# A two-layer graph network on one core: 36 instead of 28 groups of layer 1 take their rows from one-hot products, and ScalarE writes every fifth one-hot

## The chip, the core and the metric

The kernel runs on one core of one Trainium2 chip. The core has five engines that run their own instruction queues in order and wait for each other by semaphores: TensorE (PE, with its weight loads listed apart as PEld), VectorE (DVE), ScalarE (ACT), GpSimd (POOL) and SyncE (SP, which only issues transfers here). The metric is device time in microseconds (us) of one execution. Six executions of the kernel before took 3845.5 to 3851.33 us, with a median of 3848.85 us.

## What is computed

There are N = 12,500 nodes with 48 features and E = 200,000 edges, sorted by their target `dst`. Layer 0 is an edge network, layer 1 a sum of rectified messages, and each is added to its input and normalised over the features:

```python
x_i, x_j = x[dst], x[src]
h   = relu(concat([x_i, x_j, e32]) @ W1 + b1)
x   = layernorm(x + segment_sum(h @ W2 + b2, dst, N))          # layer 0
m   = relu(x[src] + e48)
x   = layernorm(x + (1 + eps) * x + segment_sum(m, dst, N))     # layer 1
```

What matters below is `x[src]` in layer 1: 200,000 rows of 48 floats, taken from 12,500 nodes in an order that the edges give.

## The kernel before, in words

The edges are cut into 391 groups of 512 (`NCHUNK` groups of `TPC` = 4 tiles of 128 edges). Layer 0 is a loop over the 391 groups, then layer 1 is another one. The instructions are written out in a fixed order by hand (`run`): in step k each stage handles group k minus its offset, and every engine meets its instructions in that order.

In layer 1 a step k issues, in this order:

- `fetch1(k+5)`: four indirect transfers on POOL's queue (L201), one for each tile, each of which brings 128 rows of `x1_dram` into the tile `xs`. The pool `cats` has 10 buffers for `xs` (`AHEAD + 5`), so the gathers of a group can start once the add of the tenth gathered group before it has been done.
- `fill1(k+2)`: DVE makes the 48-wide one-hot `hot` of the target (L302); SP loads the edge features `e48c` every fifth group.
- `sum1(k-1)`: PE multiplies messages with `hot` (L323), DVE adds the result to the window of sums `agg` (L318).
- every 28 groups a `finish1`: the sums of 896 nodes are turned, added and normalised (L331 to L357), mostly on DVE.
- `message1(k)`: DVE adds rows and edge features (`m`, L495), ACT applies the relu (`msg`, L497).
- `lead1(k)`: takes one portion from the generator `products()`.

`products()` replaces the gathers of some groups, the list `PE_GROUPS`; `fetch1` skips these. It works on two of these groups at a time (`BATCH` = 2, so `tiles` = 8 tiles). `place` makes `which` in PSUM, a bf16 tile of 128 x 1024: for each edge the number of its source's block of 128 nodes, at the row of the node within the block, and 0 elsewhere (8 DVE operations `which_e` at L515, 8 PE transposes at L520). Then, for each of the 98 blocks of nodes, `select` compares `which` with the block's number in one DVE operation of 128 x 1024 (`o`, L525), and `multiply` runs 8 matmuls of that one-hot with the block's nodes `xp` (L530), which are kept in SBUF as three bf16 pieces. The three sums (`ph`, `pm`, and one of two buffers `pt`; the other `pt` holds `which`) are opened and closed by matmuls of zeros (L538) and summed by three DVE reduces (`made`, L570). A portion is `BPS` = 4 selects for the next blocks and the multiplies of the blocks selected in the portion before. The one-hots `o` have 2 x `BPS` buffers.

With 98 blocks in portions of 4 there are 25 portions and one more for the end of the pair: 26 steps for two groups, and `EVERY` = 13 groups lie from one product group to the next. The first is group 26, the last group 377; layer 1 gathers 363 groups.

Of the kernel before, what the change touches and what calls it, by code (L numbers as in the profile page):

```python
# [24 lines left out]
F32 = mybir.dt.float32  # L25
I32 = mybir.dt.int32
BF16 = mybir.dt.bfloat16
AF = mybir.ActivationFunctionType
# [3 lines left out]
P = 128  # L32
Q = 128
# [7 lines left out]
NT = -(-N // Q)  # L41
# [14 lines left out]
AHEAD = 5  # L56
NW = 4
EC = 5
FIRST = 26
EVERY = 13  # L60
NPE = 28
BATCH = 2
PIECES = 3
BPS = 4

PE_GROUPS = [FIRST + EVERY * i for i in range(NPE)]
assert PE_GROUPS[-1] < NCHUNK and NPE % BATCH == 0

# [29 lines left out]
@with_exitstack  # L98
def gnn_kernel(
    ctx: ExitStack,  # L100
    tc: tile.TileContext,
    x: bass.AP,
    src: bass.AP,
    dst: bass.AP,
    e32: bass.AP,
    e48: bass.AP,
    w1: bass.AP,
    b1: bass.AP,
    w2: bass.AP,
    b2: bass.AP,  # L110
    eps: bass.AP,
    out: bass.AP,
):
    nc = tc.nc
    flag_pool = ctx.enter_context(tc.tile_pool(name="flag", bufs=1))
    dram = ctx.enter_context(tc.tile_pool(name="dram", bufs=1, space=bass.MemoryType.DRAM))
    flag = flag_pool.tile([1, 1], I32, name="flag")
    with ExitStack() as fast:
        windowed(fast, tc, dram, flag, x, src, dst, e32, e48, w1, b1, w2, b2, eps, out)
    misfit = nc.values_load(  # L120
        flag, engines=[mybir.EngineType.PE, mybir.EngineType.DVE, mybir.EngineType.Activation,
                       mybir.EngineType.Pool, mybir.EngineType.SP],
        min_val=0, max_val=2 * P,
    )
    with tc.If(misfit > 0), ExitStack() as slow:
        general(slow, tc, dram, x, src, dst, e32, e48, w1, b1, w2, b2, eps, out)


def windowed(ctx, tc, dram, flag, x, src, dst, e32, e48, w1, b1, w2, b2, eps, out):
    nc = tc.nc  # L130
    const = ctx.enter_context(tc.tile_pool(name="const", bufs=1))
    onehots = ctx.enter_context(tc.tile_pool(name="onehots", bufs=2 * BPS))
    cats = ctx.enter_context(tc.tile_pool(name="cats", bufs=AHEAD + 5))
    echunk = ctx.enter_context(tc.tile_pool(name="echunk", bufs=3))
    work = ctx.enter_context(tc.tile_pool(name="work", bufs=2))
# [23 lines left out]
    for t in wcats:  # L159
# [22 lines left out]
                   allow_small_or_imprecise_dtypes=True)  # L182
    iota_w = const.tile([P, W], F32, name="iota_w")
    nc.gpsimd.iota(iota_w, pattern=[[1, W]], base=0, channel_multiplier=0,
                   allow_small_or_imprecise_dtypes=True)
# [6 lines left out]
                   allow_small_or_imprecise_dtypes=True)  # L192
# [7 lines left out]
    def gather(t, table, g, j):  # L200
# [9 lines left out]
    base = const.tile([1, NCHUNK], F32, name="base")  # L210
# [10 lines left out]
        off, base, starts, op=ALU.subtract  # L221
# [22 lines left out]

    part = const.tile([P, NPE, TPC], F32, name="part")
    block = const.tile([P, NPE, TPC], F32, name="block")

    def split_src():
        first = FIRST * TPC
        some = src_i[:, first : first + (NPE - 1) * EVERY * TPC].rearrange(  # L250
            "p (i c) -> p i c", c=EVERY * TPC
        )[:, :, 0:TPC]
        last = src_i[:, PE_GROUPS[-1] * TPC : (PE_GROUPS[-1] + 1) * TPC]
        bits = node.tile([P, NPE, TPC], I32, name="bits")
        for op, by, plus, to in (
            (ALU.bitwise_and, Q - 1, 0.0, part), (ALU.logical_shift_right, 7, 1.0, block)
        ):
            nc.vector.tensor_scalar(bits[:, : NPE - 1, :], some, by, None, op0=op)
            nc.vector.tensor_scalar(bits[:, NPE - 1, :], last, by, None, op0=op)
            nc.vector.tensor_scalar(to, bits, plus, None, op0=ALU.add)  # L260
# [244 lines left out]
    tiles = BATCH * TPC  # L505
# [3 lines left out]
    def place(first):  # L509

        which = psum.tile([Q, tiles, P], BF16, name="pt", bufs=2)
        for i in range(BATCH):
            which_e = work.tile([P, TPC, Q], BF16, name="which_e")
            for j in range(TPC):
                nc.vector.tensor_scalar(  # L515
                    which_e[:, j, :], iota_q, part[:, first + i, j : j + 1],
                    block[:, first + i, j : j + 1], op0=ALU.is_equal, op1=ALU.mult,
                )
            for j in range(TPC):
                nc.tensor.transpose(which[:, i * TPC + j, :], which_e[:, j, :], ident16)  # L520
        return which

    def select(which, b):
        o = onehots.tile([Q, tiles, P], BF16, name="o")
        nc.vector.tensor_scalar(o, which, float(b + 1), None, op0=ALU.is_equal)  # L525
        return o

    def multiply(ps, o, b):
        for k in range(tiles):
            nc.tensor.matmul(  # L530
                ps[k // PER][:, k % PER, :], o[:, k, :], xp[:, b, :, :],
                start=False, stop=False, skip_group_check=True,
            )

    def edge_of(ps, start):
        for t in ps:
            n = t.shape[1] * PIECES * D
            nc.tensor.matmul(  # L538
                t.rearrange("p k c d -> p (k c d)"), zeros[:, :P], zeros[:, :n],
                start=start, stop=not start,  # L540
            )
# [4 lines left out]
    def products():  # L546

        for first in range(0, NPE, BATCH):
            due = PE_GROUPS[first]
            which = place(first)  # L550
            ps = [
                psum.tile([P, min(PER, tiles - k * PER), PIECES, D], F32, name=name,
                          bufs=2 if name == "pt" else 1)
                for k, name in enumerate(SUMS)
            ]
            edge_of(ps, True)
            last = []
            for b in range(0, NT, BPS):
                now = [(b + i, select(which, b + i)) for i in range(min(BPS, NT - b))]
                for c, o in last:  # L560
                    multiply(ps, o, c)
                last = now
                yield due
            for c, o in last:
                multiply(ps, o, c)
            edge_of(ps, False)
            xs = work.tile([P, tiles, D], F32, name="made")
            for k, t in enumerate(ps):
                n = t.shape[1]
                nc.vector.tensor_reduce(  # L570
                    xs[:, k * PER : k * PER + n, :], t.rearrange("p k c d -> p k d c"),
                    AX.X, ALU.add,
                )
            for i in range(BATCH):
                made[PE_GROUPS[first + i]] = xs[:, i * TPC : (i + 1) * TPC, :]
            yield due

    work1 = products()

    def lead1(k):  # L580
# [217 lines left out]
```

## Time and profile before

| what | value |
|---|---|
| median of six executions | 3848.85 us |
| the profiled execution | 3844.86 us |
| its span, first to last instruction | 3843.1 us |
| mean granted TensorE clock | 0.785 of full |
| layer 0 gathers, first and last start | 1564, 7.5 and 1969.9 us |
| layer 1 gathers, first and last start | 1452, 1990.5 and 3826.9 us |
| DVE selects (L525) | 1372, 677 ns each |

The page gives the busy time of each engine, its course over 40 slices of the span, and the groups of instructions by line. The timeline lists instructions in order of time with the idle time before each and what ended it. PE's busy time is modelled from pipelined matmuls and is not PE at its peak. The granted clock comes in stretches at full and at half speed, so a mean of 0.8 is a mixture of the two.

### The profile page before, as it was taken

How to read it: one execution, taken by the hardware profiler on the slowest of the kernel's cores; microseconds unless marked ns; L12 is line 12 of the kernel's file. 1: busy time of each engine (PE TensorE's matmuls, PEld its weight loads, DVE VectorE, ACT ScalarE, POOL GpSimd, SP SyncE). 2: the span in 40 equal slices, each digit the busy share in tenths (PEclk: the TensorE clock that was granted, in tenths of full speed). 3: DMA queues.
4: the chain of work that ended last, by engine and by line, in shares of the span. 5: the costliest groups of instructions: out<-in, count | busy, mean ns of one | idle time of the engine just before them, and what ended most of it. 6: DMA issues, size and time to landing. Idle time of an engine off the chain costs nothing. (4 is left out here: it accounts for less than half of the span.)

```text
span 3843.1 us, 67581 instructions
## 1 busy us (share of the span) xinstructions
PE 2857.3 (74%) x23396; PEld 2210.4 (58%) x23396; DVE 1896.1 (49%) x4618; ACT 565.2 (15%) x1329; POOL 2883.9 (75%) x3025
## 2 busy tenths in 40 slices
PE   7888888888888888888876766767676676667631
PEld 4555555556555556555556656656666665666531
DVE  3333333333333333333356766767677677767731
ACT  2222212212212212212110000000000000000000
POOL 7777777777777777777767777777777777777776
PEclk8787777787778777777778788878888888878865
DMA  2222222222212222222212222222222222212221
GB/s 71 43 45 48 43 45 46 47 40 49 48 39 45 49 41 47 49 37 47 41 40 43 45 43 38 55 45 43 38 50 43 38 50 49 44 33 55 45 43 28
DMA packets 293005, 171.68 MB, mean 45 GB/s; under 512 B 109664, under 2 KB 292400, under 8 KB 292656
## 3 DMA queue, kind: packets, MB, share of 16 engines
q0 software_dynamic: 96512, 74.31, 13.2%
q1 hardware_dynamic: 179248, 84.31, 8.1%
q10 hardware_dynamic: 16896, 8.69, 0.8%
q8 instruction: 185, 3.03, 0.3%
q14 instruction: 164, 1.34, 0.1%
HBM read 154.45 MB, written 12.62 MB: 43 GB/s over the span
## 5 line engine op out<-in xcount | busy, mean ns | idle before, releaser
L201 POOL DMA_INDIRECT cat<-in_x_dram,src_i x1564 | 1486.9, 951 | 481.4 <-issue 342.0
L201 POOL DMA_INDIRECT xs<-x_dram,src_i x1452 | 1395.1, 961 | 462.0 <-issue 339.1
L530 PEld LDWEIGHTS <-o 128*128 128x128 bf16 x10976 | 848.6, 112 | 22.9 <-DVE o L525 0.6
L525 DVE TENSOR_SCALAR o<-pt 128x1024 bf16<-128x1024 bf16 x1372 | 848.5, 677 | 5.4 <-PE pt L520 5.4
L419 DVE COPY cat_t<-pt 128x512 f32<-128x512 f32 x391 | 270.2, 691 | 898.4 <-PE pt L417 898.4
L323 PE MATMUL pa<-hot,msg 128*48 128x48 f32 x3128 | 257.5, 235 | 557.9 <-ACT msg L497 557.4
L417 PEld LDWEIGHTS pt<-ident,cat 128*128 128x128 f32 x1564 | 265.5, 176 | 631.6 <-DMA cat<-in_x_dram,src_i 365.2
L424 PE MATMUL ph<-cat_t,wcat 128*128 128x512 f32 x782 | 579.0, 831 | 0.8 <-DVE cat_t L419 0.8
L323 PEld LDWEIGHTS pa<-hot,msg 128*48 128x48 f32 x3128 | 204.5, 145 | 639.6 <-ACT msg L497 618.1
L417 PE MATMUL pt<-ident,cat 128*128 128x128 f32 x1564 | 389.9, 349 | 238.3 <-DMA cat<-in_x_dram,src_i 235.2
L530 PE MATMUL ph<-xp,o 128*128 128x144 bf16 x4116 | 565.3, 255 | 0.0
L530 PE MATMUL pm<-xp,o 128*128 128x144 bf16 x4116 | 562.8, 254 | 0.0
L432 PE MATMUL pm<-w_sb,h 128*128 128x48 f32 x3128 | 538.7, 326 | 1.3 <-ACT h L426 1.3
L432 PEld LDWEIGHTS pm<-w_sb,h 128*128 128x128 f32 x3128 | 484.8, 237 | 28.1 <-ACT h L426 2.4
L426 ACT ACTIVATE h<-ph,b_sb 128x512 f32<-128x512 f32 x391 | 269.0, 688 | 1370.5 <-PE ph L424 1351.9
L530 PE MATMUL pt<-xp,o 128*128 128x144 bf16 x2744 | 453.9, 253 | 0.0
L495 DVE TENSOR_TENSOR m<-xs,e48c 128x192 f32<-128x192 f32 x363 | 132.9, 366 | 539.6 <-DMA xs<-x_dram,src_i 539.1
L497 ACT ACTIVATE msg<-m 128x192 f32<-128x192 f32 x391 | 141.8, 363 | 1606.2 <-DVE m L495 1606.2
L323 PE MATMUL pa<-cat,msg 128*48 128x48 f32 x3128 | 263.6, 239 | 33.0 <-DVE msg L434 30.5
L323 PEld LDWEIGHTS pa<-cat,msg 128*48 128x48 f32 x3128 | 210.5, 149 | 113.1 <-issue 55.9
L434 DVE TENSOR_TENSOR msg<-pm,b_sb 128x192 f32<-128x192 f32 x391 | 139.4, 356 | 236.7 <-PE pm L432 234.6
L318 DVE TENSOR_TENSOR agg<-agg,pa 48x48 f32 x782 | 151.4, 194 | 175.2 <-PE pa L323 124.1
(79 smaller groups left out, 1064.6 us busy)
## 6 DMA issues: line engine op xcount, KB each, us to landing
e48c<-in_e_dram SPq DMA_DIRECT2D x78, 480.0 KB
cat<-in_x_dram,src_i POOLq DMA_INDIRECT x1564
e32c<-in_e_dram SPq DMA_DIRECT2D x78, 320.0 KB
xs<-x_dram,src_i POOLq DMA_INDIRECT x1452
wcat<-a SPq DMA_DIRECT2D x391, 24.0 KB
a<-a ACTq DMA_DIRECT2D x14, 256.0 KB
a<-a ACTq DMA_DIRECT2D x14, 192.0 KB
x_seg<-in_x_dram SPq DMA_DIRECT2D x14, 168.0 KB
```

The costliest lines, as they stand in the source:

```text
L201: nc.gpsimd.indirect_dma_start(out=t, out_offset=None, in_=table, in_offset=bass.IndirectOffsetOnAxis(ap=src_i[:, g * TPC + j : g * TPC + ...
L318: nc.vector.tensor_tensor(cols, cols, pa, op=ALU.add)
L323: nc.tensor.matmul(pa, msg[:, j, :], hot[:, j, :], start=j == 0, stop=j == TPC - 1)
L417: nc.tensor.transpose(pt[:, j, :], cat[g][:, j, :], ident[:P, :P])
L419: nc.vector.tensor_copy(cat_t, pt)
L424: nc.tensor.matmul(ph, wcats[g % NW], h[g], start=True, stop=True)
L426: nc.scalar.activation(t, ph, AF.Relu, bias=b1_sb)
L432: nc.tensor.matmul(pm[:, j, :], h[g][:, j, :], w2_sb, start=True, stop=True)
L434: nc.vector.tensor_tensor(msg, pm, b2_sb[:, None, :].to_broadcast([P, TPC, D]), op=ALU.add)
L497: nc.scalar.activation(msg, m, AF.Relu)
L525: nc.vector.tensor_scalar(o, which, float(b + 1), None, op0=ALU.is_equal)
L530: nc.tensor.matmul(ps[k // PER][:, k % PER, :], o[:, k, :], xp[:, b, :, :], start=False, stop=False, skip_group_check=True,)
```

## The change

Three constants give the product groups: the first is group 20, one in ten follows, 36 in all (20, 30, ... 370). A portion has 5 blocks instead of 4, so the one-hots have 10 buffers. For blocks 2, 7, ... 97 (20 of 98) ACT writes the one-hot in two operations, the square of `which` minus the block's number and then relu(1 - square), by way of one buffer `square`. The bias comes from a new constant `less`, filled by one POOL iota. The portion that ended a pair is gone: the last multiplies and the reduces now stand in the same step as the `place` and first selects of the next pair, so that a pair takes 20 steps.

```diff
-FIRST = 26
-EVERY = 13
-NPE = 28
+FIRST = 20
+EVERY = 10
+NPE = 36
-BPS = 4
+BPS = 5
+BY_ACT = 2
...
+    less = const.tile([Q, NT], F32, name="less")
+    nc.gpsimd.iota(less, pattern=[[-1, NT]], base=-1, channel_multiplier=0,
+                   allow_small_or_imprecise_dtypes=True)
+
     def select(which, b):
         o = onehots.tile([Q, tiles, P], BF16, name="o")
+        if b % BPS == BY_ACT:
+            square = work.tile([Q, tiles, P], BF16, name="square", bufs=1)
+            nc.scalar.activation(square, which, AF.Square, bias=less[:, b : b + 1])
+            nc.scalar.activation(o, square, AF.Relu, bias=1.0, scale=-1.0)
+            return o
         nc.vector.tensor_scalar(o, which, float(b + 1), None, op0=ALU.is_equal)
         return o
...
                 made[PE_GROUPS[first + i]] = xs[:, i * TPC : (i + 1) * TPC, :]
-            yield due
```

## The prediction

> **What bounds the kernel now.** I read the page first, its busy line and its slices.
>
> ```profile
> PE 2857.3 (74%) x23396; PEld 2210.4 (58%) x23396; DVE 1896.1 (49%) x4618; ACT 565.2 (15%) x1329; POOL 2883.9 (75%) x3025
> DVE  3333333333333333333356766767677677767731
> POOL 7777777777777777777767777777777777777776
> ```
>
> POOL is at the same 7 tenths in both layers, though PE and DVE change by a factor of two between them. That speaks for a fixed pace on POOL. The groups of instructions confirm it:
>
> ```profile
> L201 POOL DMA_INDIRECT xs<-x_dram,src_i x1452 | 1395.1, 961 | 462.0 <-issue 339.1 <-DMA xs<-x_dram,src_i 86.6 <-DVE o L525 15.5
> L525 DVE TENSOR_SCALAR o<-pt 128x1024 bf16<-128x1024 bf16 x1372 | 848.5, 677 | 5.4 <-PE pt L520 5.4
> L426 ACT ACTIVATE h<-ph,b_sb 128x512 f32<-128x512 f32 x391 | 269.0, 688 | 1370.5 <-PE ph L424 1351.9
> ```
>
> A gather takes 0.96 us and is followed by 0.3 us of issue, whatever it is put down to; a POOL that waited for others would show long gaps. In layer 1 the starts run from 1990.53 to 3826.92: 1836.4 us over 1451 intervals, 1.2656 each, 5.062 for a group. Next, the list of waits: DVE's add waits for the gathered rows in 270 of 363 cases.
>
> ```profile
> DVE m L495 <- DMA xs<-x_dram,src_i: 539.1, 270, 4.2
> ```
>
> So DVE has slack, and the question is how much. The timeline of DVE shows it where DVE is behind and works without a pause, and at the change from one pair to the next:
>
> ```profile
> 2284.63 0.35 DVE L495 TENSOR_TENSOR m<-xs,e48c 128x192 f32<-128x192 f32 x1
> 2284.90 2.48 DVE L525 TENSOR_SCALAR o<-pt 128x1024 bf16<-128x1024 bf16 x4
> 2287.30 0.34 DVE L302 TENSOR_TENSOR hot<-iota_w,rel 128x192 f32<-128x192 f32 x1
> 2287.56 0.19 DVE L318 TENSOR_TENSOR agg<-agg,pa 48x48 f32 x1
> 2287.68 0.34 DVE L495 TENSOR_TENSOR m<-xs,e48c 128x192 f32<-128x192 f32 x1
> ```
> ```profile
> 2585.65 0.39 DVE L495 TENSOR_TENSOR m<-xs,e48c 128x192 f32<-128x192 f32 x1 [2.26 <-DMA xs<-x_dram,src_i]
> 2585.96 0.59 DVE L570 TENSOR_REDUCE made<-ph 128x144 f32<-128x432 f32 x1
> ...
> 2587.36 0.34 DVE L302 TENSOR_TENSOR hot<-iota_w,rel 128x192 f32<-128x192 f32 x1
> ...
> 2591.51 2.13 DVE L515 TENSOR_SCALAR which_e<-iota_q,part,block 128x128 bf16<-128x128 f32 x8
> 2594.03 2.48 DVE L525 TENSOR_SCALAR o<-pt 128x1024 bf16<-128x1024 bf16 x4 [0.39 <-PE pt L520]
> ```
>
> A step with four selects lasts 3.05 us from add to add, against 5.06 for the gathers of a group. The four selects overlap: 2.40 from the first's start to `hot`, 0.60 apart.
>
> **The change, part by part.** *Gathers.* 363 gathered groups become 355: 32 gathers less, 32 x 1.2656 = **40.5 us less on POOL**, the path that sets the end. This is the whole gain.
>
> *The iota* (`less`) stands on POOL before layer 1's first gather. The nearest row, an iota of 128x128, took 0.24 us, and POOL idles 19.72 us there until the last of `x1_dram` is written. Nothing; uncovered it would cost 0.3.
>
> *ACT instead of DVE for 20 of 98 blocks.* DVE still has 4 selects a step. The built program's semaphores decide what ACT's part does to it: the Square waits for the DVE select before it, and the next DVE select waits for the Square, because both engines read the one PSUM tile `which`. So ACT does not work beside DVE here: DVE stands still during the Square, and behind the waiting select stand the fourth select, `hot`, `agg` and the next add, for which ACT's relu, PE's sums and, ten gathered groups on, POOL wait. Only the Relu lies beside DVE.
>
> The price of a Square has no row. The nearest in kind is L426, PSUM to SBUF with a pointer bias, 0.688 for 512 elements; the copies from PSUM took 0.597 for 512 and 0.491 for 384, a slope of 0.83 ns an element. From L426: 0.688 + 512 x 0.00083 = 1.112. Low end, from the copy: 0.597 + 0.424 = 1.021. High end, by the slope from L497 (192 elements, 0.363) to L426, 1.016 ns: 1.208. I take 1.112, since L426 differs only in length and type. The handovers are 0.09 (add to relu, DVE to ACT) and 0.03 (ACT to DVE), both in the chain of waits at the end. A step then grows by 0.09 + 1.11 + 0.03 and by 0.08 of lost overlap (0.677 less 0.60): 1.32. **DVE's step becomes 4.37.**
>
> The Trainium skill, "PSUM — Partial Sum Buffer", section "PSUM bank collisions raise a hardware error", speaks against this change: accesses of two engines to one bank and quadrant have to be kept apart by semaphores, two reads too. No row of before shows two engines reading one tile, so this trace can't confirm it; if reads could lie beside each other, the sum would end at the 40.5 gained. The skill's "ScalarE: Activation LUTs", section "What ACT_TABLE_LOAD costs", gives about 280 ns plus 0.833 ns an element for a pointer bias, an estimate of 1.133 for the Square; L426 at 0.688 agrees with it within 3%, and the sum below would be 7 us longer by it.
>
> *A round of 20 steps on DVE.* Eighteen steps of 4.37 are 78.6. The step with blocks 95 to 97 has two DVE selects and nothing behind its Square: 3.05 - 2 x 0.60 = 1.85. The next, which ends a pair and begins another: the reduces wait for PE, PE for block 97 from ACT. Square and Relu are through 3.85 after the add before, so 2.0 after this one; 8 matmuls and the zeros add about 1.1: 3.1. Then 1.40 for the reduces (2585.96 to 2587.36), 2.52 to the first select (2591.51 to 2594.03), and 5 blocks with `hot` and `agg`: 2.40 + 0.38 + 1.32 = 4.10. In all 11.1. Round: **91.6**, plus a `finish1` every 28 steps, 5.4 and 5.9 in two places of the timeline, 5.6 taken. POOL needs 18 x 5.062 = 91.1. DVE, which had some 30% to spare, becomes as slow as POOL or slower.
>
> *What becomes of it.* Call lag the time from landing to add. Before, group 0 has 7.7 (its last gather starts at 1994.4, lands 2.5 later, its add starts at 2004.6). Six portions stand before it, each 1.32 longer: 15.6. Fourteen steps take off 0.69 each, the short step 3.2, the long one adds 6.1: 8.8 at group 16. From there to 341, the last group before the final round thins out: DVE 16 x 91.6 + 5 x 4.37 + 12 finishes x 5.6 = 1555; POOL gathers 325 - 33 = 292 groups, 1478. The lag would reach 86. But 10 buffers hold it: a group's gathers begin ten groups, 50.6, after those of the group whose buffer they take, of which 3.8 to its last start, 2.5 to landing and 0.4 for the add are used. Room 44. So **POOL stands still for 42 us**. After step 355 there are no selects and the rest is gathered at the old pace.
>
> *Waits for PE.* In the 113 steps of before without idle time ahead of the add, DVE lost 8.4 us ahead of `agg`, 0.07 each. PE gets 40 instead of 32 matmuls a step, but 4.37 instead of 3.05 us for them: 0 to 0.07, or 0 to 24 us over 325 steps. I take 7.
>
> **Sum: -40.5 + 42 + 7 = +8.5.** The profiled execution's 3844.9 would become 3853; against the median, which is 4 us above it, **3857 us**.
>
> **The rivals.** *Gain kept.* If Square and selects lay beside each other, a DVE round is 66.5 plus 4 for finishes, far under 91.1, no lag grows and the time is 3848.85 - 40.5 = 3808. For it: ACT is 15% busy, and only one Square a step is in question. Against it: the semaphores. Short of that, 329 Squares count from the start to group 341, so the Square would have to cost 0.15 less, 0.96, below my low end, for POOL never to wait. Chance 0.15.
>
> *PE at half clock* (L530, slower). The matmuls follow each other at 62 ns at full clock and 120 at half. A round is 784 of them, 20 sums at 0.56 and about 2 us of the rest: 62 us at full, over 120 at half. It passes DVE's 95 when the granted clock is under 0.65; at 0.6 a round is 103 and 17 rounds cost 200, less the room, about +120, 3970. For it: the throttle granted 0.73 to 0.83 in layer 0's middle, with PE busier. Against: layer 1 had 0.82 with PE waiting for DVE and rows, and its stretch from 2600 us was granted 0.86 at 72% busy, that from 2500 0.76 at 69%. More work raises the clock there. Chance 0.05.
>
> *Dearer operations*: selects that get slower beside the Relu, or a Square above my bound. At 0.05 more for each of 78 selects, 17 rounds cost 66: 3923. For it: nothing measured; against it: selects keep 669 to 692 ns while PE, ACT and POOL work. Chance 0.10.
>
> **How the numbers follow.** The forecast has 0.70. Its own bounds: each 0.1 us of the Square is 33 us, so 1.021 gives -30 and 1.208 gives +32, with the PE waits -7 to +17: 3820 to 3906. That holds 0.70 at most, so the range reaches down to the kept gain: 3806 to 3906. Left out are the two dear rivals, 0.15. What can be told from no change is 0.2%, 3841.2 to 3856.5. The forecast lies just above: 0.18 below, 0.17 within, 0.35 above. With the kept gain's 0.15 below and the two dear rivals' 0.15 above: faster 0.33, same 0.17, slower 0.50.
>
> **What would show it.** Right: DVE idle ahead of selects, released by ACT, some 350 times and about 1.2 us each; add to add 4.3 to 4.4; POOL gaps released by DVE's add, 20 to 80 us in all, late in layer 1; a granted clock above 0.85 there. Wrong: DVE's idle time still put down to gathers, or PE's weight loads without gaps. The number is wrong first if the Square or a round is mis-sized: 1 us a round is 17.

## The result, and the profile after

The changed kernel took 3858.36 us (median of 17 executions, 3856.37 to 3861.61), the kernel before 3847.14 us (37 executions, 3839.9 to 3851.33). The ratio is 1.0031, with a 95% interval of 1.0024 to 1.0037. So the change costs 11 us, where the forecast had 8. In seven of the runs reported below the kernel before itself took 4838 to 4930 us (medians), so their times are compared only with the kernel before that ran beside them.

| | before | after |
|---|---|---|
| profiled execution, span | 3844.86, 3843.1 us | 3857.11, 3855.2 us |
| mean granted TensorE clock | 0.785 | 0.848 |
| layer 1 gathers | 1452 | 1420 |
| their first and last start | 1990.5, 3826.9 us | 1986.1, 3839.0 us |
| POOL stops for DVE's add longer than 0.32 us | none | 25, 69.3 us |

On the page of the changed kernel I read the busy line and the slices of DVE, POOL and the granted clock.

```profile
PE 2949.9 (77%) x26588; PEld 2260.8 (59%) x26588; DVE 1939.5 (50%) x4694; ACT 1344.9 (35%) x2049; POOL 2847.5 (74%) x2994
DVE  3333333333333333333347777777777777777751
POOL 7777777777777777777767777777776777777676
PEclk9787777777787777777789999999999999999975
```

DVE is at 7 tenths throughout layer 1, where before it went up and down between 6 and 7. POOL, which was at 7 from the start of layer 1 to the end, now shows a 6 in two more slices of the last third: there it waits. The groups of instructions and the list of waits (total us, times, longest) say for what.

```profile
L202 POOL DMA_INDIRECT xs<-x_dram,src_i x1420 | 1359.6, 957 | 510.6 <-issue 368.7
L535 DVE TENSOR_SCALAR o<-pt 128x1024 bf16<-128x1024 bf16 x1404 | 899.1, 680 | 432.8 <-ACT square L532 425.8
L540 PEld LDWEIGHTS <-o 128*128 128x128 bf16 x14112 | 917.5, 101 | 440.3 <-ACT o L533 418.2
L532 ACT ACTIVATE square<-pt,less 128x1024 bf16<-128x1024 bf16 x360 | 401.2, 1114 | 395.3 <-DVE o L535 395.3
```
```profile
DVE o L535 <- ACT square L532: 425.8, 342, 1.5
POOL xs L202 <- DVE m L496: 72.0, 34, 5.6
DVE m L496 <- DMA xs<-x_dram,src_i: 51.1, 17, 3.9
```

The three waits form a chain. DVE's selects wait 342 times for the Square, 1.24 us each. DVE's add waits for gathered rows only 17 times instead of 270: its slack is used up. And POOL waits for the add to give buffers back. Nine of those 34 waits are the usual 0.3 us that is there between two gathers anyway; the other 25 are real stops, 69.3 us in all and 61.7 us beyond that 0.3.

DVE's timeline (start, length, engine, line; in brackets the idle time before and what ended it) shows one step and then the change from one pair to the next.

```profile
3030.09 0.34 DVE L496 TENSOR_TENSOR m<-xs,e48c 128x192 f32<-128x192 f32 x1
3030.36 1.27 DVE L535 TENSOR_SCALAR o<-pt 128x1024 bf16<-128x1024 bf16 x2
3032.88 1.29 DVE L535 TENSOR_SCALAR o<-pt 128x1024 bf16<-128x1024 bf16 x2 [1.24 <-ACT square L532]
...
3034.46 0.34 DVE L496 TENSOR_TENSOR m<-xs,e48c 128x192 f32<-128x192 f32 x1
...
3036.39 0.36 DVE L496 TENSOR_TENSOR m<-xs,e48c 128x192 f32<-128x192 f32 x1
3039.35 0.61 DVE L580 TENSOR_REDUCE made<-ph 128x144 f32<-128x432 f32 x1 [2.60 <-PE ph L548]
...
3043.27 1.29 DVE L535 TENSOR_SCALAR o<-pt 128x1024 bf16<-128x1024 bf16 x2 [0.38 <-PE pt L521]
```

Add to add is 3034.46 - 3030.09 = 4.37 us, with the stop in the middle of the selects; the step of blocks 95 to 97 is 3036.39 - 3034.46 = 1.93. At the change of the pair the reduces wait for PE, as the forecast's working had it. POOL's timeline shows what a late add does to the gathers:

```profile
3099.16 0.95 POOL L202 DMA_INDIRECT xs<-x_dram,src_i  x1 [0.30 <-issue]
3103.35 0.95 POOL L202 DMA_INDIRECT xs<-x_dram,src_i  x1 [3.24 <-DVE m L496]
```

The add that it waited for started at 3102.73, right behind a `finish1`. The six stops of over 4 us all come there, where DVE does something besides the selects.

**The account.** From first to last gather start layer 1 takes 1852.9 us instead of 1836.4, 16.5 more: 40.5 less for 32 gathers, 61.7 more for the stops, and some 5 less because this execution's gathers were a little shorter. Layer 1 began 4.4 us earlier in this execution, and behind the last gather nothing changed: 16.5 - 4.4 = 12.1, the difference of the spans. The gain came in full and was given back as stops.

### The profile page after: what moved, and what is told of

It is laid out like the page before. It is cut to its first block, busy times and chain, and to the rows that moved or that the text cites. A ratio compares the mean times of both kernels' runs of the same rounds, so it can differ in the third digit from the quotient of the medians.

```text
span 3855.2 us, 75307 instructions
## 1 busy us (share of the span) xinstructions
PE 2949.9 (77%) x26588; PEld 2260.8 (59%) x26588; DVE 1939.5 (50%) x4694; ACT 1344.9 (35%) x2049; POOL 2847.5 (74%) x2994
## 5 line engine op out<-in xcount | busy, mean ns | idle before, releaser
L202 POOL DMA_INDIRECT xs<-x_dram,src_i x1420 | 1359.6, 957 | 510.6 <-issue 368.7
L540 PEld LDWEIGHTS <-o 128*128 128x128 bf16 x14112 | 917.5, 101 | 440.3 <-ACT o L533 418.2
L535 DVE TENSOR_SCALAR o<-pt 128x1024 bf16<-128x1024 bf16 x1404 | 899.1, 680 | 432.8 <-ACT square L532 425.8
L540 PE MATMUL ph<-xp,o 128*128 128x144 bf16 x5292 | 648.0, 233 | 356.7 <-ACT o L533 356.2
L540 PE MATMUL pm<-xp,o 128*128 128x144 bf16 x5292 | 640.3, 232 | 0.0
L532 ACT ACTIVATE square<-pt,less 128x1024 bf16<-128x1024 bf16 x360 | 401.2, 1114 | 395.3 <-DVE o L535 395.3
L540 PE MATMUL pt<-xp,o 128*128 128x144 bf16 x3528 | 523.9, 231 | 0.0
L533 ACT ACTIVATE o<-square 128x1024 bf16<-128x1024 bf16 x360 | 380.4, 1057 | 11.4
L324 PE MATMUL pa<-hot,msg 128*48 128x48 f32 x3128 | 235.8, 223 | 125.4 <-ACT msg L498 125.4
L324 PEld LDWEIGHTS pa<-hot,msg 128*48 128x48 f32 x3128 | 185.4, 133 | 183.2 <-ACT msg L498 135.9
```

What stands on the lines that cost most here:

```text
L202: nc.gpsimd.indirect_dma_start(out=t, out_offset=None, in_=table, in_offset=bass.IndirectOffsetOnAxis(ap=src_i[:, g * TPC + j : g * TPC + ...
L324: nc.tensor.matmul(pa, msg[:, j, :], hot[:, j, :], start=j == 0, stop=j == TPC - 1)
L532: nc.scalar.activation(square, which, AF.Square, bias=less[:, b : b + 1])
L533: nc.scalar.activation(o, square, AF.Relu, bias=1.0, scale=-1.0)
L540: nc.tensor.matmul(ps[k // PER][:, k % PER, :], o[:, k, :], xp[:, b, :, :], start=False, stop=False, skip_group_check=True,)
```

## The experiments

The theory: the Square and the selects share the PSUM tile `which` and take turns, so DVE's step grows, the adds fall behind, and ten buffers no longer hold the delay. Rivals: ACT's work costs by being there at all; the 36 groups cost more on PE than they save; selects get dearer. Under each kernel the medians come first, each with that of the kernel before beside it, their ratio and its 95% interval.

**All one-hots on DVE.** DVE writes five one-hots a step, ACT none; the 36 groups stay.

```diff
-BY_ACT = 2
+BY_ACT = -1
```

> 36 groups as in the change, but DVE makes all 98 one-hots of a pair. Theory (DVE stands still while ACT squares, and its rounds outlast POOL's): a step has five selects and no stop, 3.05 + 0.60 = 3.65 us from add to add instead of 4.37; a round of 20 steps is 18 x 3.65 + 2.45 + about 9 + 5 for finishes = 82 us against 91 for POOL's gathers. DVE falls behind nowhere for long, POOL's gaps from DVE's add vanish, and the 40 us of the gathers are kept: 3807 us. Rival 1 (the 40 matmuls a step on PE set the pace): DVE waits for PE ahead of agg and the time stays near 3858. Rival 2 (fewer gathers are worth nothing because something else paces POOL): 3847.

> The same kernel as in e1_dve_only, 36 groups with all one-hots made by DVE, again, since the kernel before itself took 4930 us there. If the kernel before takes its 3847 us here: theory (DVE's stop during the Square is the cost) 3807 us, no gap of POOL released by DVE's add, a step of 3.65 us. Rival 1 (40 matmuls a step on PE set the pace): near 3858. Rival 2 (fewer gathers are worth nothing): 3847. If the kernel before is slow again, every engine's pauses will be there again, and nothing is told apart.

> The kernel of e1_dve_only (36 groups, DVE makes all 98 one-hots of a pair) on a chip where, it is hoped, the kernel before takes its 3847 us. Theory (DVE's stop during the Square makes its rounds outlast POOL's): without it a step is 3.65 us, a round 82 against 91: no POOL gap released by DVE's add, 3807 us. Rival 1 (40 matmuls a step on PE set the pace): near 3858. Rival 2 (fewer gathers are worth nothing): 3847.

e1_dve_only took 5029.41 beside 4929.57 (1.0214, 1.0182 to 1.0247), e1b_dve_only 4929.12 beside 4853.98 (1.0176, 1.0133 to 1.0219). e1c_dve_only took **3802.61 us** (3801.08 to 3804.04) beside 3847.47: 0.9883, 0.9867 to 0.99. From the list of waits and the timeline of DVE in e1c_dve_only:

```profile
DVE m L496 <- DMA xs<-x_dram,src_i: 264.6, 167, 4.9
```
```profile
3003.89 0.36 DVE L496 TENSOR_TENSOR m<-xs,e48c 128x192 f32<-128x192 f32 x1 [0.94 <-DMA xs<-x_dram,src_i]
3004.17 3.08 DVE L535 TENSOR_SCALAR o<-pt 128x1024 bf16<-128x1024 bf16 x5
...
3007.54 0.34 DVE L496 TENSOR_TENSOR m<-made,e48c 128x192 f32<-128x192 f32 x1
```

Five selects on DVE alone make a step of 3.65 us, less than the 4.37 with four selects and a Square, and under the 5.06 of a group's gathers. The add waits for rows again (167 times), no wait of POOL for DVE's add is longer than the usual 0.3 us, and the layer 1 gathers run from 1990.8 to 3786.1, which is 1795.3 us: 41.1 less than before, against 40.5 worked out. So the groups alone are worth 45 us in the median, and ACT's part of the change costs 3858.36 - 3802.61 = 56 on top of them.

**ACT takes the last block of a portion.** The Square now comes behind the DVE selects of its step; ACT writes 19 blocks of 98 instead of 20.

```diff
-BY_ACT = 2
+BY_ACT = 4
```

> As the change, but ACT writes the last one-hot of each portion instead of the third (blocks 4, 9, ... 94, 19 instead of 20). The same operations on ACT, the same semaphores. Theory: the Square now lies beside hot, agg and the next add, so DVE's stop ahead of a select shrinks from 1.24 to about 0.67 us, a step is 3.7 us, a round about 84 against POOL's 91: 3807 us. Rival (ACT's two operations are too dear in themselves, or reach PE too late): stays near 3858.

> The kernel of e2_act_last (ACT takes the last one-hot of each portion instead of the third, same operations, same semaphores) again. Theory: the Square lies beside hot, agg and the next add; DVE's stop ahead of a select shrinks from 1.24 to about 0.67 us, a step is 3.7 us, a round about 84: 3807 us. Rival (ACT's two operations are too dear in themselves, or reach PE too late): near 3858.

e2_act_last: 4982.53 beside 4929.57 (1.0122, 1.0084 to 1.016). e2b_act_last: **3791.29 us** (3790.64 to 3791.73) beside 3847.47: 0.9856, 0.9839 to 0.9872. From its list of waits and its timeline:

```profile
DVE o L535 <- ACT square L532: 112.2, 192, 1.3
```
```profile
3001.71 0.35 DVE L496 TENSOR_TENSOR m<-xs,e48c 128x192 f32<-128x192 f32 x1
3002.65 2.48 DVE L535 TENSOR_SCALAR o<-pt 128x1024 bf16<-128x1024 bf16 x4 [0.60 <-ACT square L532]
...
3005.44 0.34 DVE L496 TENSOR_TENSOR m<-xs,e48c 128x192 f32<-128x192 f32 x1
```

The turn-taking is still there, but `hot`, `agg` and the next add read other tiles and run beside the Square; some 0.6 us of it is left as a stop, and only where DVE is behind (192 waits, 112.2 us). The step is 3.73. It was 16 us faster than the 3807 expected of it, and the theory does not account for that. Its profiled execution is 13.3 us shorter than that of e1c_dve_only: its gathers started every 1.2585 us against 1.2652 there (1419 intervals, 9.5 us), and those of layer 1 began 4.1 us earlier. Why gathers get shorter or longer is taken up below.

**ACT reads its own copy of `which`.** ACT does the same work as in the changed kernel, from SBUF; DVE makes the copy once a pair (692 ns).

```diff
+            own[0] = work.tile([Q, tiles, P], BF16, name="own")
+            nc.vector.tensor_copy(own[0], which)
...
-            nc.scalar.activation(square, which, AF.Square, bias=less[:, b : b + 1])
+            nc.scalar.activation(square, own[0], AF.Square, bias=less[:, b : b + 1])
```

> As the change, but DVE copies which once per pair from PSUM into SBUF, and ACT squares that copy. Nothing of ACT's shares a tile with DVE's selects any more. Theory: no select waits for a Square, a step is 3.05 us, a round about 73 with the copy of 0.7: 3807 us, and DVE's idle time is put down to gathers again. Rival (ACT's reads and writes slow DVE even without a semaphore): selects get longer than 680 ns and the time lies between 3807 and 3858.

> The same kernel as in e3_own_copy (ACT squares a copy of which in SBUF, made by DVE once per pair), again, since the kernel before took 4930 us beside it. If the kernel before takes its 3847 us here: theory (the cost is DVE's stop during the Square, which the shared tile brings) 3807 us, no select waits for a Square, steps of 3.05 us when DVE is behind. Rival (ACT's work slows DVE even without a semaphore, or reaches PE too late): between 3807 and 3858. If the kernel before is slow again, nothing is told apart by the times.

> The kernel of e3_own_copy (ACT squares a copy of which in SBUF that DVE makes once per pair) again. Theory (the stop comes with the shared tile): no select waits for a Square, steps of 3.05 us when DVE is behind, 3807 us. Rival (ACT's work slows DVE even without a semaphore): selects longer than 680 ns, between 3807 and 3858.

e3_own_copy: 4976.6 beside 4929.57 (1.011, 1.0076 to 1.0144). e3b_own_copy: 4953.98 beside 4890.62 (1.0104, 1.0052 to 1.0156). e3c_own_copy: **3802.71 us** (3799.07 to 3807.33) beside 3847.47: 0.9889, 0.9872 to 0.9905. Three lines of DVE's timeline and, below them, one of ACT's:

```profile
3003.81 0.36 DVE L496 TENSOR_TENSOR m<-xs,e48c 128x192 f32<-128x192 f32 x1 [3.42 <-DMA xs<-x_dram,src_i]
3004.09 2.48 DVE L537 TENSOR_SCALAR o<-pt 128x1024 bf16<-128x1024 bf16 x4
...
3006.86 0.34 DVE L496 TENSOR_TENSOR m<-made,e48c 128x192 f32<-128x192 f32 x1
```
```profile
3004.53 1.13 ACT L534 ACTIVATE square<-own,less 128x1024 bf16<-128x1024 bf16 x1
```

The Square, from 3004.53 to 3005.66, lies inside the four selects. No select waits for it, and the selects are as long as ever (679 ns against 680). The step is back at 3006.86 - 3003.81 = 3.05 us. This is the direct test: 360 Squares and 360 Relus as in the changed kernel, without the shared tile, and 56 us less. ACT's work costs nothing by being there; taking turns on the tile, with ten buffers for the rows, costs all of it.

**Twenty buffers for the rows.** The turn-taking stays, the room doubles.

```diff
-        cat[g] = cats.tile([P, TPC, D], F32, name="xs")
+        cat[g] = cats.tile([P, TPC, D], F32, name="xs", bufs=20)
```

> As the change, with 20 instead of 10 buffers for the gathered rows. Theory (POOL stops only because the lag of DVE outgrows the ten buffers): ten more hold 50.6 us more of lag; of the 61.6 us that POOL stood still 11 remain, at the very end of the rounds; steps stay at 4.37 us: 3858 - 50.6 = 3808 us. Rival (DVE's rounds set the end whatever the buffers): stays near 3858.

> The same kernel as in e4_bufs20 (20 instead of 10 buffers for the gathered rows), again, since the kernel before took 4930 us beside it. If the kernel before takes its 3847 us here: theory (POOL stops only because DVE's lag outgrows ten buffers) 11 us of POOL's stops remain and the time is 3808 us, with steps of 4.37 us as in the change. Rival (DVE's rounds set the end whatever the buffers): near 3858. If the kernel before is slow again, nothing is told apart by the times.

e4_bufs20: 5039.9 beside 4929.57 (1.0225, 1.0189 to 1.026). e4b_bufs20: **3806.36 us** (3804.97 to 3806.85) beside 3841.47: 0.991, 0.9893 to 0.9926. From its list of waits:

```profile
DVE o L535 <- ACT square L532: 424.2, 341, 1.5
POOL xs L202 <- DVE m L496: 25.8, 29, 5.6
PEld L540 <- ACT o L533: 421.6, 328, 1.6
```

DVE stands still for the Square as long as in the changed kernel, and PE's weight loads wait for ACT's one-hots as long (421.6 us against 418.2), and yet 52 us are gone (46 when each kernel is taken against the kernel before that ran beside it). So neither wait costs time by itself: what DVE's delay costs is decided by the room for it. 6 stops are left, 17.0 us beyond the usual 0.3, and the first begins at 3454 instead of 2680 us. The time from a group's last gather start to its add reaches 106 us, where ten buffers had held it at 54. The 3808 expected was met in number, with 17 us of stops for the 11 expected; the kernel before beside it was 6 us faster than elsewhere.

**ACT's part without the eight groups.** The 28 groups and portions of 4 of the kernel before, with ACT writing every fourth block.

```diff
+BY_ACT = 2
...
+        if b % BPS == BY_ACT:
+            square = work.tile([Q, tiles, P], BF16, name="square", bufs=1)
+            nc.scalar.activation(square, which, AF.Square, bias=less[:, b : b + 1])
+            nc.scalar.activation(o, square, AF.Relu, bias=1.0, scale=-1.0)
+            return o
```

> The kernel before, 28 groups in steps of 13 and portions of 4, with ACT's two operations alone added: blocks 2, 6, ... 94 of a pair, every fourth, with the shared tile. Theory (the stop costs only where DVE's round outlasts POOL's): a step is 3.05 - 0.60 + 1.32 = 3.77 us, a round of 26 steps 24 x 3.77 + about 6 + 6 for finishes and new windows = 103 us against 24 x 5.06 = 121 for POOL, so DVE stops some 330 times for 1.24 us, 410 us in all, and the time stays at 3847. Rival (ACT's operations cost by themselves, through PE's late one-hots or slower gathers): slower by 0.3% or more.

4880.8 us beside 4837.59: 1.0081, 1.0053 to 1.0109. It doesn't answer its question: beside a kernel before of some 3847 us ACT's part alone was not tried.

**More groups with what was learned.** 46 groups, one in 8 from group 16; portions of 7 with one block on ACT, which reads its own copy; two steps without selects at the end of a pair.

```diff
-FIRST = 20
-EVERY = 10
-NPE = 36
-BPS = 5
-BY_ACT = 2
+FIRST = 16
+EVERY = 8
+NPE = 46
+BPS = 7
+BY_ACT = (2,)
...
+            own[0] = work.tile([Q, tiles, P], BF16, name="own", bufs=1)
+            nc.vector.tensor_copy(own[0], which)
...
+            yield due
+            yield due
```

> A version that is meant to beat both: the SBUF copy of e3, 46 product groups (one in eight, a round of 16 steps for a pair), portions of 7 blocks of which ACT makes one, and two steps of a round without selects. 345 groups are gathered instead of 363. Theory (POOL's gathers set the end as long as DVE's round is shorter): a round is 84 x 0.60 + 16 x 0.65 + about 7 + 4 for finishes = 72 us on DVE against 14 x 5.06 = 71 on POOL, so lag stays within the ten buffers: 3847 - 18 x 5.06 = 3756 us, some us more where the lag touches the room. Rival (PE, with 56 matmuls in a step, sets the pace): above 3800.

**3773.92 us** (3768.98 to 3775.1) beside 3847.47: 0.9806, 0.9789 to 0.9822, the lowest time of all. From its list of waits, and then the gathers' groups of x46 and of e2b_act_last:

```profile
POOL xs L202 <- DVE m L496: 6.1, 20, 0.3
```
```profile
L202 POOL DMA_INDIRECT xs<-x_dram,src_i x1380 | 1349.1, 978 | 436.4 <-issue 314.5
```
```profile
L202 POOL DMA_INDIRECT xs<-x_dram,src_i x1420 | 1354.1, 954 | 448.7 <-issue 324.3
```

POOL never stopped, as expected, but the 3756 expected were missed by 18 us. The gathers themselves got longer: 978 ns against 954, and 1768.6 us / 1379 = 1.2825 from start to start against the 1.2656 of the kernel before. 1379 x 0.0169 = 23 us, more than the whole miss.

**Where PE pauses.** In e1_dve_only, e1b_dve_only, e2_act_last, e3_own_copy, e3b_own_copy and e4_bufs20 the kernels with 36 groups took 1 to 2% longer than the kernel before beside them, those with all one-hots on DVE and with twenty buffers most. That is the opposite of what the same kernels did in e1c_dve_only, e2b_act_last, e3c_own_copy and e4b_bufs20. In the traces of those six and of e5_act_13 PE falls behind already in layer 0, whose code is the same in all: in 131 to 153 of its 391 groups ACT's `h` waits more than 1 us after PE's last modelled matmul for it, up to 20 us, together 528 to 598 us; in the profile of before this happens 13 times, 45 us. Instructions of DVE, ACT and POOL last as long as elsewhere. What makes PE pause there was not found, and why these kernels took longer than the kernel before there stays open. The account above rests on the other runs alone.

## Why the prediction was right, step by step

**What bounds the kernel.** Right. With POOL never stopped (all on DVE) 32 gathers less gave 41.1 us between first and last gather start; 40.5 were worked out. One reading on the way was loose: between the layers DVE's slices double, but PE's go only from 8 tenths to 6 or 7.

**The Square and the step.** Right to the hundredth: the Square took 1.114 us (1.112 worked out from the relu of layer 0), DVE stopped 342 times (some 350), the step is 4.37 (4.37). Its mechanism, two readers of one PSUM tile taking turns, is shown by the own copy, which keeps all of ACT's work and has steps of 3.05. The Trainium skill, "ScalarE: Activation LUTs", section "What ACT_TABLE_LOAD costs", gave an estimate of 1.133: 2% over the Square from PSUM at 1.114, and met by the Square from SBUF in e3c_own_copy at 1.133. The rule that the forecast cited from "PSUM — Partial Sum Buffer", section "PSUM bank collisions raise a hardware error", is what the program's semaphores do here, and it cost 56 us; what two unguarded readers would do was not tried.

**The round.** Short step 1.89 to 1.93 (1.85), pair change 11.0 to 11.3 (11.1; two behind a `finish1` in the short step took 8.4 and 8.3), `finish1` 5.2 to 5.9 (5.6): all close. But one part of DVE's work was left out. Every 28 groups DVE clears a new window of sums:

```profile
2134.97 0.34 DVE L496 TENSOR_TENSOR m<-xs,e48c 128x192 f32<-128x192 f32 x1
...
2139.48 0.98 DVE L314 MEMSET agg<- 48x1104 f32 x1 [0.17 <-issue]
...
2140.76 0.36 DVE L496 TENSOR_TENSOR m<-xs,e48c 128x192 f32<-128x192 f32 x1
```

That step is 2140.76 - 2134.97 = 5.79 instead of 4.37, 1.42 more (1.45 in most such places), and 12 of them lie between groups 16 and 341: 17 us. DVE took 1570.4 us there (2082.52 to 3652.90), 1555 were worked out.

**The lag and the room.** Right in kind: the first stop begins at 2680 us, all stops lie behind the first third of layer 1. The term that was mis-sized is **"POOL stands still for 42 us"**: it measured 61.7. At group 0 the lag was 14.4 us (15.6): five portions stand before its add, not six, and 7.7 + 5 x 1.32 = 14.3. At group 16 it was 9.6 (8.8), since the first window is cleared in between. From there to group 341 DVE took 1570.4 us, and POOL without its stops 1474.1 (1478). So the lag would have reached 106 instead of 86, and less the room of 44 that makes the 62 that were measured. Twenty buffers, which cut the stops to 17.0, show that it is the room that turns DVE's delay into time.

**Waits for PE, 7 us.** Not there. DVE's waits for PE's sums ahead of `agg` were 39.8 us in layer 1, 44.6 before. This term, the shorter gathers (5 us) and the earlier start (4 us) of this execution stand against 20 us more of stops. That 3857 was forecast and 3858.36 measured is luck to that extent: the mechanism was right, the size of its main term by a third too small.

**The rivals.** The kept gain needed a Square and selects side by side; that is e3c_own_copy, 3802.71, where the rival had 3808. PE at half clock: the opposite came, as the fences on the clock below show, and PE's weight loads idle 418.2 us for ACT's one-hots. The two stretches that the forecast gave against this rival were a thin ground: in the same trace that from 2300 us had 0.86 at 66% busy and that from 2400 us 0.82 at 72%. Dearer selects: 680 ns against 677.

## What to carry to other kernels

Before an idle engine is given part of a busy one's work, ask which tile both read: if semaphores make them take turns, the operation moved adds its whole length to the busy engine, and an operand of one's own (here a 0.69 us copy every 20 steps) or a place in the order where the other has different work removes that. An engine with slack may be slowed for nothing up to the point where its round passes that of the bound, and beyond that the buffers decide when the delay is paid; count every operation of the round for this, the rare ones too. Try a change's parts apart: here one was worth -45 us and the other cost 56 on top of it.

## What the runs showed of the hardware

**PE's clock rose with more matmuls.** From 2100 to 3600 us, before and then after (length; busy time and count of PE, PEld, DVE, ACT, POOL; granted clock, DMA share, GB/s):

```profile
2100.00:3600.00 1500.00, 1047.63 (x12473) 935.37 (x12474) 1057.86 (x2437) 125.42 (x344) 1139.43 (x1184) 0.82 0.22 44
```
```profile
2100.00:3600.00 1500.00, 1107.94 (x15016) 960.49 (x15014) 1068.42 (x2436) 796.38 (x957) 1096.88 (x1147) 0.95 0.22 43
```

With 20% more matmuls the clock went from 0.82 to 0.95, and PE's busy time grew by only 6%. The forecast had said above 0.85. The number of matmuls alone does not set the clock: in the same stretch e1c_dve_only had 15834 of them at 0.91 and x46 19340 at 0.92.

In the trace of before the clock changes only after multiples of 3.41 us. Take windows of that length between 2100 and 3600 us that were at full clock: after each of the 72 in which PE was busy, by the modelled matmuls, for less than 0.4 of the time the clock was halved, and after 176 of the 177 with more than 0.5 it stayed full. In layer 0 that bound does not hold: of 62 such windows with 0.5 to 0.7 busy only 10 were followed by full clock. So these traces show no one busy share that keeps the clock.

**Gathers lengthen beside DVE's add.** From start to start they averaged 1.2585 us in e2b_act_last, 1.2652 in e1c_dve_only, 1.2656 in before and 1.2825 in x46. In x46, 234 of 1380 gathers took over 1.0 us, 1.44 at most. Of the 113 in which an add of DVE (`m`) began 0.2 to 0.3 us after the gather's own start, 110 did, with a mean of 1.162 us; of the 979 with no add that began from 0.4 us before the gather to its end, 20 did, with a mean of 0.949. In before it was 7 of 14 against 59 of 1057. That is a correlation, and no run took the add away. The Trainium skill, "SBUF — State Buffer", section "Who interferes with whom", states that a DVE instruction with two inputs in SBUF, as the add and `hot` are, contends with a GpSimd instruction that reads SBUF. Whether a gather counts as one no run here shows, and the same section tells of a probe in which a `tensor_tensor` did not stall DMA, so the cause stays open. If it is DVE's add, then DVE's work is not free for POOL even where POOL never waits for it.
